# Perceiver block on one core: score maxima from half of the contraction rows, four heads side by side, three iterations a unit, one ring of five PSUM banks

## The chip, the cores and the metric

The kernel runs on one core of one Trainium2 chip. A core has a matrix engine (TensorE, PE in the profile; its weight loads are shown as PEld), a vector engine (VectorE, DVE), a scalar engine (ScalarE, ACT), a general one (GpSimd, POOL) and a queue engine (SyncE, SP) that issues the transfers (DMAs). Each engine takes its instructions in order and waits on semaphores for the others. SBUF is the working memory, with 128 partitions (rows); PSUM takes the results of matmuls, in eight banks of 512 fp32 numbers a partition. The metric is the device time of one execution in microseconds (us). The kernel before took 3726.22 us, the median of three runs (3722.47 to 3727.96).

## What is computed

Two perceiver layers run over `x` (32 batches, 64 latents, width 256). Each begins with a cross attention to a context of 32 x 1601 rows, with 16 heads of 16 numbers; the second one has a mask. Self attentions and feed-forward blocks follow. The part that the change touches is the cross attention:

```
def _L0_xattn_ref(q, k, v, wq, bq, wk, bk, wv, bv, wo, bo):
    qh = (q @ wq + bq).reshape(b, -1, H, HD).transpose(0, 2, 1, 3)
    kh = (k @ wk + bk).reshape(b, -1, H, HD).transpose(0, 2, 1, 3)
    vh = (v @ wv + bv).reshape(b, -1, H, HD).transpose(0, 2, 1, 3)
    scores = jax.nn.softmax(jnp.einsum('bhqd,bhkd->bhqk', qh, kh), axis=-1)
    attn = jnp.einsum('bhqk,bhkd->bhqd', scores, vh)
    concat = attn.transpose(0, 2, 1, 3).reshape(b, -1, H * HD)
    return concat @ wo + bo
...
x = x + _L0_xattn_ref(_layernorm(x, axis=-1), ctx_1024, ctx_1024, ...)
x = x + _L0_attn_ref(...)
x = x + _L0_ffn_ref(...)
x = x + _L1_xattn_ref(_layernorm(x, axis=-1), ctx_1024, mask_BxS2_ik0, ...)
x = x + _L1_attn_ref(...)
x = x + _L1_ffn_ref(...)
```

## The kernel before

The method `stream` does both cross attentions in one loop and puts the smaller blocks of layer 0 between its steps. The order of the instructions is written by hand: what the Python code emits first stands first on each engine.

**Units.** A unit `u` is one batch and four of its heads (`b, q4 = divmod(u, 4)`); with two layers of 32 batches there are 256. For each unit the keys of four heads are fetched, the maximum of each row of scores is found, the exponents of (score minus maximum) are made, and the values are summed with them.

**Exact products from bf16 parts.** A key or a query number is split into three bf16 parts (0, 1, 2, from coarse to fine). The contraction over a head's 16 numbers becomes one over 6 x 16 = 96 rows, which hold six products of parts: `PARTS` says which part of the key each sixth row has, `QPARTS` which part of the query. Row 16 and so on belong together by a step of six: `k[s : 96 : 6]`. Rows from 96 hold constants: ones against the maximum's two bf16 parts, and in layer 1 the mask row.

**What a unit runs**, by the functions that the change touches:

- `fetch(u)` (L1145) loads the key tile `kst` from `kd`, the keys' parts in HBM, with six transfers, one for each sixth row (L1154), and one more for the constant rows (L1158). The pool `kst` has three tiles: `fetch(u + 2)` stands at the head of unit `u` and waits until unit `u - 1` has read its tile.
- `maxima(u)` (L1169) makes the scores once with queries on the partitions: 32 queries of a head in each of four column groups of PE, 96 rows (97 in layer 1), 400 keys to a matmul (L1182). Each set of four fills one bank `sp` (a pool of three), which DVE reduces (L1187). Eight sets make a unit. Then `neg`, `mm` (L1190 to L1192) and a transposing matmul `rp` into a bank of the ring `tp` (L1196), and ACT copies the maxima from there into rows 96 and on of the query tile `qst` (L1200).
- `probabilities(u, i)` (L1206) makes the scores again with keys on the partitions, now with the maximum subtracted by the extra rows (98 or 99 rows), two chunks of 128 keys to a bank `tp` (L1217; a ring of two banks, shared with `rp`), and ACT takes the exponent (L1222). Seven calls make a unit.
- `weighted(u, i, e)` (L1225) sums the values into the bank `acc`, 17 columns of PE to a head (L1232).

**What runs between.** `keys_values` makes the keys and values of later batches, one bank at a time: `kp` (12 matmuls, L1048, evacuated by DVE at L1054) and `vp` (12, L1076, evacuated by ACT at L1081), 13 banks for four units. They use two banks in turn, `mm0` and `mm1`, as do the group and end steps (`group_step`, `end_step`: queries, self attention, the feed-forward block, the finish of a batch pair). `parted` (L989) splits the keys with ACT and POOL and stores them to `kd`; `split` (L939) casts a context tile (`chi`, ACT) and makes its rest (`clo`, POOL). `tick` (L962) emits pending pieces of these, at most two pieces of work at each call, and issues the context loads that were asked for one tick before. All loads and stores go through SP's queue.

**The loop.** A unit has four iterations. Each issues part of the next unit's maxima (3, 3, 3 steps, and in the fourth `rp`), the sums of the iteration before, two exponents' scores, a group step, a tick, projections up to a target, and an end step:

```
for i in range(4):
    for _ in range((3, 3, 3, 0)[i]):
        next(nat, None)
    for done in late:
        weighted(*done)
    ...
    late = [(u, j, probabilities(u, j)) for j in range(2 * i, min(2 * i + 2, 7))]
    ...
    keys_values(LEAD + (4 * u + i + 1) / 16.0, 0.15)
    end_step()
```

**The start.** Before the loop, `stream` loads the first context tiles (six of them into a key tile that is not yet needed, `early`), makes the first queries with a layer norm whose reciprocal root runs on POOL (`rsqrt`, L196), and the keys of batch 0. DVE's cast of the value weights (L204) stands behind that layer norm's L533 in DVE's order.

Of the kernel before, what the change touches and what calls it, by code (L numbers as in the profile page):

```python
# [19 lines left out]
F32 = mybir.dt.float32  # L20
F32R = mybir.dt.float32r
BF16 = mybir.dt.bfloat16
# [19 lines left out]
PARTS = (0, 0, 0, 1, 1, 2)  # L42
QPARTS = (0, 1, 2, 0, 1, 0)
# [15 lines left out]
class Kernel:  # L59
# [188 lines left out]
    def stream_setup(self, wp, bg, bank):  # L248
# [39 lines left out]
        self.eye = wp.tile([P, NQ], F32, tag="eye", name="eye")  # L288
# [7 lines left out]
        self.tri = wp.tile([P, NQ], F32, tag="tri", name="tri64")  # L296
# [34 lines left out]
        for c0 in (0, half):  # L331
# [7 lines left out]
            nc.sync.dma_start(self.rows[:, 0, c0 : c0 + n], mf[:, :n])  # L339
# [134 lines left out]

    def stream(self):
        nc, tc, ins = self.nc, self.tc, self.ins
        with ExitStack() as ctx:
# [6 lines left out]
            kq = pool("kq", 2)  # L484
            kp_ = pool("kst", 3)
            vp_ = pool("v")
            pt = pool("pt", 2)
# [5 lines left out]
            ps_n = pool("psn", 3, space=PSUM)  # L493
            ps_t = pool("pst", 2, space=PSUM)
            ps_m = pool("psm", 1, space=PSUM)
# [3 lines left out]

            self.rows = dram.tile([NB, 3, NKP], BF16, tag="rows", name="rows")  # L500
# [7 lines left out]
            def nrows(b):  # L508

                return (96, 98) if layer(b) == 0 else (97, 99)  # L510


            banks = [0, 0]

            def bank(name):
                banks[0] += 1
                banks[1] ^= 1
                return ps_m.tile([P, 512], F32, tag=f"mm{banks[1]}", name=name)
# [44 lines left out]
            def queries(n, g):  # L563
# [27 lines left out]
                q = kq.tile([P, 16, 2 * P], BF16, tag="qst", name=f"{name}_qst{g}")  # L591
                for s, part in enumerate(QPARTS):
                    nc.sync.dma_start(
                        q[s : 96 : 6], qd[part].rearrange("(h d) n -> d h n", d=16)
                    )
                if n == 1:
                    nc.sync.dma_start(
                        q[96:97],
                        self.rows[0:1, 1, : 2 * P].unsqueeze(1).to_broadcast([1, 16, 2 * P]),
                    )  # L600
# [388 lines left out]
            def parted(i, x, quick):  # L989
# [6 lines left out]
                nc.scalar.copy(ks[:, 0, :, :m], upper(x))  # L996
                eng.tensor_tensor(x, x, upper(x), ALU.subtract)  # L997
# [6 lines left out]
                if not quick:  # L1004

                    yield "wait"
# [134 lines left out]
            mms = [wp.tile([P, 2, 3], BF16, tag=f"mm{r}", name=f"mm_{r}") for r in range(4)]  # L1141
            for mm in mms:
                nc.gpsimd.memset(mm[:, :, 0:1], 1.0)

            def fetch(u):  # L1145

                b, q4 = divmod(u, 4)
# [1195 lines left out]
```

## Time and profile before

| | |
|---|---|
| median of three runs | 3726.22 us |
| the profiled execution | 3724.4 us |
| its span, first to last instruction | 3722.7 us |
| mean granted TensorE clock | 0.959 |
| maxima: `sp` matmuls, L1182 | 8192, 511.9 us busy |
| scores for the exponents: `tp`, L1217 | 13312, 580.3 us |
| sums: `acc`, L1232 | 26624, 580.4 us |
| exponents on ACT, L1222 | 1792, 933.7 us |
| reductions on DVE, L1187 | 2048, 1049.7 us |
| key loads | 1536 of 201.0 KB |

Busy times of PE overlap: its matmuls are pipelined, and those in different column groups run side by side, so the sum of the rows is more than PE's share. For the cost of a group of matmuls the start of one is compared with the start of the next. "Idle before" with a releaser says how long an engine had nothing to do before a group, and what ended that.

By stage:

```
us            PE busy  DVE    ACT    POOL   clock  DMA share
0-60          37.63    31.88  23.50  16.53  0.96   0.62
60-460        380.88   246.42 254.37 191.14 0.97   0.82
1260-1660     391.03   248.93 258.32 194.51 1.00   0.76
2460-2860     385.42   242.29 265.94 214.64 0.99   0.85
2860-3160     283.46   179.42 190.62 146.73 0.97   0.82
3160-3722     418.56   465.24 255.51 162.99 0.81   0.05
```

### The profile page before, as it was taken

To read this page: it belongs to the slowest core of one execution; us is meant where nothing else is said; L and a number is where in the kernel's file an instruction comes from. 1 tells how busy PE (TensorE), PEld (TensorE's weight loads), DVE (VectorE), ACT (ScalarE), POOL (GpSimd) and SP (SyncE) were. 2 spreads that over 40 slices of the span, in tenths; PEclk is the share of its full clock that TensorE was granted. 3 is DMA by queue.
4 is the path that set the end of the run, shared out by engine and by line. 5 is a ranking of instruction groups with operands and counts; after the bars stand their busy time and mean duration, and the time that the engine had idled before them with its cause. 6 is when DMAs were issued, how large, how long until landed. Compare 5 with 4: busy or idle time off the path is not lost. (4 is left out here: it accounts for less than half of the span.)

```text
span 3722.7 us, 154775 instructions
## 1 busy us (share of the span) xinstructions
PE 3471.3 (93%) x66591; PEld 2817.5 (76%) x66591; DVE 2437.7 (65%) x6161; ACT 2290.3 (62%) x4400; POOL 1747.7 (47%) x2113
## 2 busy tenths in 40 slices
PE   7999999999999999999999999999999999675698
PEld 6788888888888888878887888788888787342467
DVE  5666666655665666666766666665656565689879
ACT  4666666666666666666666666566666665244662
POOL 3444445545554445544555555555555553003246
PEclk9999999999999999999999999999999999786699
DMA  7887777777877787867877787778888887200000
GB/s 187 229 222 204 195 192 206 207 189 189 206 191 194 188 207 194 217 176 186 206 191 194 181 200 195 195 190 215 219 211 213 213 220 188 73 1 1 1 5 20
DMA packets 669950, 643.36 MB, mean 173 GB/s; under 512 B 114448, under 2 KB 567376, under 8 KB 669136
## 3 DMA queue, kind: packets, MB, share of 16 engines
q1 hardware_dynamic: 669264, 633.45, 66.6%
q8 instruction: 523, 8.57, 1.0%
q14 instruction: 163, 1.34, 0.1%
HBM read 462.30 MB, written 170.98 MB: 170 GB/s over the span
## 5 line engine op out<-in xcount | busy, mean ns | idle before, releaser
L1187 DVE TENSOR_REDUCE mx<-sp 128x1 f32<-128x400 f32 (+1 forms) x2048 | 1049.7, 566 | 415.9 <-PE sp L1182 412.6
L1222 ACT ACTIVATE e<-tp 128x512 f32<-128x512 f32 (+1 forms) x1792 | 933.7, 566 | 594.7 <-PE tp L1217 585.1
L997 POOL TENSOR_TENSOR kr<-kr 128x512 f32<-128x512 f32 (+1 forms) x406 | 411.8, 1014 | 932.3 <-ACT ks L996 853.3
L1054 DVE TENSOR_SCALAR kr<-kp,bk 128x256 f32<-128x256 f32 (+1 forms) x832 | 356.6, 470 | 546.3 <-PE kp L1048 430.0
L944 POOL TENSOR_TENSOR clo<-raw,chi 128x512 fp32r<-128x512 f32 (+1 forms) x408 | 509.6, 1249 | 415.7 <-ACT chi L943 407.7
L1232 PEld LDWEIGHTS acc<-e,v 128*17 128x17 f32 x26624 | 459.0, 98 | 196.7 <-ACT e L1222 78.3
L1232 PE MATMUL acc<-e,v 128*17 128x64 f32 x26624 | 580.4, 221 | 29.0 <-ACT e L1222 19.5
L1217 PE MATMUL tp<-xa_qst,kst 98*128 98x64 bf16 (+2 forms) x13312 | 580.3, 195 | 0.0
L1182 PE MATMUL sp<-kst,xa_qst 96*32 96x400 bf16 (+3 forms) x8192 | 511.9, 343 | 51.8 <-DMA kst<-kd 19.2
L1217 PEld LDWEIGHTS <-kst 98*128 98x128 bf16 (+2 forms) x13312 | 460.1, 100 | 111.8 <-issue 3.6
L1076 PE MATMUL vp<-w_hi,chi 128*128 128x256 f32 (+1 forms) x1664 | 509.0, 306 | 11.9 <-DVE w_hi L204 9.5
L1076 PE MATMUL vp<-w_lo,chi 128*128 128x256 f32 (+1 forms) x1664 | 471.8, 284 | 0.4 <-DVE w_lo L205 0.3
L1076 PE MATMUL vp<-w_hi,clo 128*128 128x256 f32 (+1 forms) x1664 | 471.0, 283 | 0.0
L998 POOL TENSOR_TENSOR ks<-kr 128x512 bf16<-128x512 f32 (+1 forms) x406 | 412.2, 1015 | 31.8
L1048 PE MATMUL kp<-chi,w_hi 128*128 128x256 f32 (+1 forms) x1664 | 373.1, 306 | 7.1 <-DVE w_hi L204 5.6
L1081 ACT COPY v<-vp 128x512 f32<-128x512 f32 (+1 forms) x416 | 244.4, 587 | 165.7 <-PE vp L1076 155.0
L1076 PEld LDWEIGHTS vp<-w_hi,chi 128*128 128x128 f32 (+1 forms) x1664 | 311.9, 187 | 32.7 <-issue 10.3
L1048 PE MATMUL kp<-chi,w_lo 128*128 128x256 f32 (+1 forms) x1664 | 336.5, 284 | 0.1
L1048 PE MATMUL kp<-clo,w_hi 128*128 128x256 f32 (+1 forms) x1664 | 334.2, 283 | 1.3 <-POOL clo L944 1.3
L996 ACT COPY ks<-kr 128x512 bf16<-128x512 bf16 (+1 forms) x416 | 252.3, 607 | 121.8 <-DVE kr L1054 109.7
L1076 PEld LDWEIGHTS vp<-w_lo,chi 128*128 128x128 f32 (+1 forms) x1664 | 312.3, 188 | 1.5 <-DVE w_lo L205 0.9
L1182 PEld LDWEIGHTS <-xa_qst 96*32 96x32 bf16 (+1 forms) x8192 | 155.5, 95 | 206.6 <-issue 97.4
(721 smaller groups left out, 5245.8 us busy)
## 6 DMA issues: line engine op xcount, KB each, us to landing
kst<-kd SPq DMA_DIRECT2D x1536, 201.0 KB
kd<-ks SPq DMA_DIRECT2D x384, 384.0 KB
raw<-in_ctx_dram SPq DMA_DIRECT2D x379, 256.0 KB
xa_qst<-xa_qd SPq DMA_DIRECT2D x96, 128.0 KB
kd<-ks SPq DMA_DIRECT2D x64, 108.0 KB
xa_qd<-xa_qs SPq DMA_DIRECT2D x16, 384.0 KB
kst<-rows SPq DMA_DIRECT2D x128, 37.7 KB
raw<-in_ctx_dram SPq DMA_DIRECT2D x62, 72.0 KB
```

Source lines behind the costliest of these rows:

```text
L944: (nc.vector if i < 2 else nc.gpsimd).tensor_tensor(lo[:, :, :n], raw[:, :, :n], hi[:, :, :n].bitcast(F32), ALU.subtract)
L996: nc.scalar.copy(ks[:, 0, :, :m], upper(x))
L997: eng.tensor_tensor(x, x, upper(x), ALU.subtract)
L998: eng.tensor_tensor(ks[:, 2, :, :m], x, upper(x), ALU.subtract)
L1048: nc.tensor.matmul(kp[:, oc, :m], wk[w][:, cc, oc * P : (oc + 1) * P], x[:, cc, :m], start=(j == 0), stop=(j == 5),)
L1054: nc.vector.tensor_scalar(r[:, oc, :m], kp[:, oc, :m], self.bk[n][:, oc : oc + 1], None, ALU.add,)
L1076: nc.tensor.matmul(vp[:w_, i1, :], x[:, cc, o], wv[w][:, cc, :], start=(j == 0), stop=(j == 5),)
L1182: nc.tensor.matmul(sp[32 * w : 32 * w + 32, :n], q[:NR, h0 + 2 * p + w // 2, t0 : t0 + 32], k[:NR, 2 * p + w // 2, k0 : k0 + n], start=Tru ...
L1187: nc.vector.tensor_reduce(mx[:, p, g : g + 1], sp[:, :n], AX.X, ALU.max)
L1217: nc.tensor.matmul(sp[:m, c, h, :], k[:NA, h, k0 : k0 + m], q[:NA, h0 + h, tok], start=True, stop=True,)
L1222: nc.scalar.activation(e[:m, :two], sp[:m, :two], AF.Exp)
L1232: nc.tensor.matmul(acc[32 * h : 32 * h + 17, slot, :], vs[b, c][:m, 4 * q4 + h, :], e[:m, c - 2 * i, h, :], start=(c == 0), stop=(c == NCH ...
```

## The change

- The maxima use 64 rows of each head's contraction instead of 96 or 97: three products of parts (0 with 0, 0 with 1, 1 with 0 in an order that differs by half) and the constant rows. Even heads use rows 0 to 63, odd heads rows 64 to 127, so that two heads' products stand in the upper half of PE and two in the lower, in two banks. A quad of matmuls has 64 queries of each of four heads and 400 keys; four quads make a unit. The maxima used for the exponents are then those of the coarser scores.
- The rows of the key and query tiles are laid out anew (`ROWS`, `PARTS`, `QPARTS`): in each half 0 to 31 by twos, 1 to 31 by twos, 35 to 50. Where the even and odd heads need different parts, a load is cut in two. All 128 rows enter the scores for the exponents. Unused rows must be zero and constant rows one, so three key tiles and two query tiles are made once and cleared at the start (two key tiles and the query tiles by POOL; the third key tile's rows by four loads in its first fetch). The mask row is loaded in layer 1 alone.
- The loop has three iterations a unit: two quads in each of the first two, `rp` in the third. Exponents 0 and 1, 3 and 4, 5 and 6 are issued as before; 2 is issued after the first iteration's projections. Group and end steps come before the tick and the projections; the third iteration has a second group step, and in odd units an end step.
- The PSUM pools of three (`sp`) and two (`mm0`, `mm1`) banks become one ring of five; the pool of exponents has three tiles instead of two.
- `parted` takes the first part by a rounding copy instead of the upper half of the bits, and stores one step earlier.

```
-PARTS = (0, 0, 0, 1, 1, 2)
-QPARTS = (0, 1, 2, 0, 1, 0)
+ROWS = [slice(r + a, r + b, c) for r in (0, 64) for a, b, c in ((0, 32, 2), (1, 32, 2), (35, 51, 1))]
+MAXR, MASKR = slice(96, 98), slice(34, 99, 64)
+PARTS = ((0, 0), (0, 2), (1, 1), (0, 0), (2, 0), (1, 1))
+QPARTS = ((0, 2), (1, 0), (0, 1), (2, 0), (0, 1), (1, 0))
...
-            pt = pool("pt", 2)
+            pt = pool("pt", 3)
-            ps_n = pool("psn", 3, space=PSUM)
-            ps_m = pool("psm", 1, space=PSUM)
+            ps_m = pool("psm", 5, space=PSUM)
...
             def bank(name):
                 banks[0] += 1
-                banks[1] ^= 1
-                return ps_m.tile([P, 512], F32, tag=f"mm{banks[1]}", name=name)
+                return ps_m.tile([P, 512], F32, tag="mm", name=name)
...
+                q = qring[g % 2]
+                for x, (r, two) in enumerate(zip(ROWS, QPARTS)):
+                    for a, part in enumerate(two):
+                        nc.sync.dma_start(
+                            parity(q[r])[a],
+                            qd[part].rearrange("(j a d) n -> a d j n", a=2, d=16)[a],
+                        )
+                    if x % 2:
+                        yield
+                nc.sync.dma_start(q[MAXR], q[51:53])
...
-                nc.scalar.copy(ks[:, 0, :, :m], upper(x))
-                eng.tensor_tensor(x, x, upper(x), ALU.subtract)
+                nc.scalar.copy(ks[:, 0, :, :m], x)
+                eng.tensor_tensor(x, x, ks[:, 0, :, :m], ALU.subtract)
...
-                if not quick:
-                    yield "wait"
                 yield "store"
...
+                k = kring[u % 3]
+                if u == 2:
+                    for r in (slice(32, 35), slice(51, 64), slice(96, 99), slice(115, P)):
+                        nc.sync.dma_start(k[r], kring[0][r])
+                for r, two in zip(ROWS, PARTS):
+                    rows = [
+                        kds[b][part, 64 * q4 : 64 * q4 + 64, :NKE] for part in two
+                    ]
+                    if two[0] == two[1]:
+                        nc.sync.dma_start(k[r], rows[0].rearrange("(h d) n -> d h n", d=16))
+                        continue
+                    for a, x in enumerate(rows):
+                        nc.sync.dma_start(
+                            parity(k[r])[a],
+                            x.rearrange("(j a d) n -> a d j n", a=2, d=16)[a],
+                        )
+                if layer(b) == 1:
+                    nc.sync.dma_start(
+                        k[MASKR],
+                        self.rows[b % NB, :NKE].unsqueeze(0).unsqueeze(0)
+                        .to_broadcast([2, 4, NKE]),
+                    )
...
+                for g, (k0, n) in enumerate(NATGROUPS):
+                    sp = [bank(f"sp{u}_{a}_{g}") for a in range(2)]
+                    for a in range(2):
+                        r = slice(64 * a, 64 * a + 64)
+                        for j in range(2):
                             nc.tensor.matmul(
+                                sp[a][64 * j : 64 * j + 64, :n], q[r, h0 + 2 * j + a, tok],
+                                k[r, 2 * j + a, k0 : k0 + n], start=True, stop=True,
                             )
+                    for a in range(2):
+                        nc.vector.tensor_reduce(
+                            mx[:, a, g : g + 1], sp[a][:, :n], AX.X, ALU.max
+                        )
+                    if g < 3:
                         yield
...
+            for k in kring[:2]:
+                nc.gpsimd.memset(k, 0.0)
+                nc.gpsimd.memset(k[MAXR], 1.0)
+            for q in qring:
+                nc.gpsimd.memset(q, 0.0)
+                for a in range(2):
+                    nc.gpsimd.memset(
+                        q[32 + 64 * a : 35 + 64 * a].rearrange("p (j a) n -> p j a n", a=2)[:, :, a],
+                        1.0,
+                    )
...
-                for i in range(4):
-                    for _ in range((3, 3, 3, 0)[i]):
+                for i, js in enumerate(((0, 1, 2), (3, 4), (5, 6))):
+                    for _ in range((2, 2, 0)[i]):
                         next(nat, None)
...
-                    if i == 3:
+                    if i == 2:
                         next(nat, None)
-                    late = [
-                        (u, j, probabilities(u, j)) for j in range(2 * i, min(2 * i + 2, 7))
-                    ]
+                    late = [(u, j, probabilities(u, j)) for j in js[:2]]
                     banks[0] = 0
                     group_step()
+                    end_step()
                     tick()
-                    keys_values(LEAD + (4 * u + i + 1) / 16.0, 0.15)
-                    end_step()
+                    keys_values(LEAD + (3 * u + i + 1) / 12.0, 0.15)
+                    late += [(u, j, probabilities(u, j)) for j in js[2:]]
+                    if i == 2:
+                        group_step()
+                        if u % 2:
+                            end_step()
```

## The prediction

> **What bounds the kernel now.** I read the page's busy shares first, then the busy time by windows, then what TensorE (PE) waits for, then one unit on the timeline. A unit is one batch and four heads; the main loop runs 256 of them.
>
> ```profile
> PE 3471.3 (93%) x66591; PEld 2817.5 (76%) x66591; DVE 2437.7 (65%) x6161; ACT 2290.3 (62%) x4400; POOL 1747.7 (47%) x2113
> 860.00:1260.00 400.00, 394.61 (x8045) 326.53 (x8043) 251.47 (x592) 260.17 (x522) 198.57 (x225) 0.99 0.76 196
> ```
>
> In the window (its columns: PE, PEld, DVE, ACT, POOL, granted clock, DMA share, GB/s) PE is busy 394.6 of 400 us, DVE 63%, ACT 65%, the DMA engines 76%. The loop runs from the first maxima at 57.85 us to about 3,172 us: 3,114 us / 255 = 12.2 us a unit. PE sets it. The remaining 550 us are not edited.
>
> ```profile
> L1182 PE MATMUL sp<-kst,xa_qst 96*32 96x400 bf16 (+3 forms) x8192 | 511.9, 343 | 51.8 <-DMA kst<-kd 19.2
> 1002.19 0.28 PE L1196 MATMUL rp<-identb,mm 128*2 128x128 bf16 x2
> 1002.40 0.32 PE L1217 MATMUL tp<-xa_qst,kst 98*65 98x64 bf16 x4
> ...
> 1004.16 0.70 PE L1182 MATMUL sp<-kst,xa_qst 96*32 96x401 bf16 x12
> 1004.69 0.28 PE L1232 MATMUL acc<-e,v 65*17 65x64 f32 x8
> 1004.91 0.64 PE L1217 MATMUL tp<-xa_qst,kst 98*128 98x64 bf16 x16
> ```
>
> The timeline's first columns are start and length. Matmuls overlap, so I cost them by start to next start. Twelve `sp` take 4.16 to 4.69, 0.53 us: 0.177 us for each set of four side by side. From `tp` to `sp` costs about 0.09 us more than staying in `tp` (start to start 123 ns against 29), from `acc` to `tp` as much.
>
> **The quads (gain).** Before, 8 sets of four a unit; after, 4 quads of 64x64 tiles, two row halves by two column halves. Do four such tiles overlap? L1629 is the same arrangement (both row halves, both column halves, two banks):
>
> ```profile
> L1629 PE MATMUL sa_dm<-sa_qk 64*64 64x64 bf16 x512 | 9.3, 228 | 8.5 <-DVE sa_mxd L1638 6.8 <-ACT sa_fi@s L1597 1.7
> ```
>
> Its starts in the trace come in fours within some 15 ns, a new four every 53 ns, so they do overlap, and 53 ns of weight loading hides under a 400-column stream. I take 0.177 us a quad: 4 x 0.177 = 0.71 us a unit, x255 = -181 us. Bounds: nothing (halves in turn) to -181. Mode switches: eight a unit before (in and out, four iterations); after, three in each of two iterations (into `sp`, `sp` to `acc`, out) and two in the third, eight again: nothing. `tp` on 128 rows instead of 98 costs nothing: 98 and 99 rows both go at 29 ns.
>
> **Wait A (cost).** The third iteration now issues `rp`, `tp` 5, `tp` 6. All three draw on the two-bank ring, so `tp` 6 needs the bank that `rp` filled, and ACT must copy it out first (L1200, 366 ns). Before, `rp` was followed by `tp` 6 alone. From the second `rp` matmul's start to the end of that copy the trace has 622 ns; ACT to a waiting PE takes 52. PE arrives at 149 (`rp` to `tp`) + 8 x 29 = 381. Stall 674 - 381 = 0.29 us a unit: +75 us (0 to 90). Queued behind it on PE are the projections and the next unit's maxima.
>
> **Wait B (cost).** `tp` 2 moves behind the projection and its exponent is used one `sp` run later. If a value projection came just before (97 of 256 units by the changed instruction order), ACT evacuates `vp` first: 904 ns after the last `vp` start, + 597 (mean exponent) + 52 = 1.55 us. PE arrives after 120 + 326 (`tp` 2 and switch) + 177 + 256 (quads, switch) + 416 (32 `acc`) = 1.30. Stall 0.26 x 97 = +25 us. After a key projection the two arrive together; I add 0.08 x 144 = 12. Sum +37 (0 to 100, if ACT has a copy queued in every unit).
>
> **Waits that go (gain).**
>
> ```profile
> PE acc L1232 <- ACT e L1222: 15.5, 28, 1.6
> ...
> PEld acc L1232 <- ACT e L1222: 70.5, 186, 1.8
> ```
>
> `acc` waits on exponents mostly where an iteration has no projection (72 of some 770). With 13 banks over 12 iterations instead of 16 nearly each has one. By start-to-start excess these stalls are 38 us; I take -25 (0 to -38). The three-bank `sp` ring costs some 22 us beside DMA waits; the five-bank ring frees -10 (0 to -22). VectorE's eight 566 ns reductions stay, 4.5 us a unit, in two bursts of four (2.3 us) inside iterations of some 3.9 us; `neg` and `mm` follow and are needed 0.3 to 0.8 us later, behind the key projection's 0.9 us evacuation if there is one. I cost that at nothing; with the cover gone it is 0.3 us a unit.
>
> **Start (cost).** GpSimd (POOL) now clears two key and two query tiles before its first useful instruction.
>
> ```profile
> L302 POOL MEMSET v<- 128x1024 f32 x1 | 1.0, 957 | 0.0
> L282 POOL MEMSET blk<- 128x128 f32 x1 | 0.2, 203 | 0.0
> ...
> 12.89 0.24 POOL L196 TENSOR_SCALAR xa_rs_v<-xa_mv 128x2 f32<-128x2 f32 x1 [10.22 <-DVE xa_mv L527]
> ...
> 16.20 0.58 PE L1076 MATMUL vp<-w_hi,chi 128*128 128x256 f32 x1 [7.51 <-DVE w_hi L204]
> ```
>
> (957 - 203) / 896 = 0.84 ns an element and about 0.1 us each. 4 x 6,432 + 2 x 4,096 + 4 x 2,048 = 42,112 elements: 35.4 + 1.0 = 36.4 us, from 2.66 to 39. The first layer norm's L196 waited only until 12.89; behind it stand, in order, DVE's L533, the cast that the first `vp` waits for, and PE. +26 us. No row has bf16 on POOL; at a quarter of the price it is hidden, so 0 to +29. Twice as many query loads at 0.63 us on SP before the first key load: 0 to +4, I take 2. Start: +28.
>
> The Trainium skill ("VectorE: DVE Perf Modes", "Zero memsets can be issued as uint32 (trn2)") says that a memset takes a cycle an element whatever the type, and that zeros can go as 4-byte words; it speaks of the Vector engine. If that were done here, the zero tiles would halve and the start cost some 18 us.
>
> **Loads (cost, and the largest doubt).**
>
> ```profile
> 1002.75 4.01 SPq L1154 DMA_DIRECT2D kst<-kd  x6
> 1006.81 0.44 SPq L1158 DMA_DIRECT2D kst<-rows  x1
> 1007.36 0.93 SPq L1009 DMA_DIRECT2D kd<-ks  x1
> ```
>
> A unit's key tile goes from 6 loads and one for rows to 8, and a mask load in layer 1: 4.5 us of SP becomes 5.4 to 6.0, and stores and context loads behind it come later. The packets end 7.1 us after the first issue (8.0 with the rows); the maxima that read them start a median 3.8 us after that. So the loads themselves stay hidden. Context loads lose cover too: three ticks a unit instead of four put the cast of a load 0.79 units after its issue point, not 0.98 (positions in the two instruction orders): 9.6 us becomes the cover instead of 12, with the issue some 1 us later. Query loads, 12 and one instead of 6 every 16 units, pass SP in groups of four, 2.5 us each, within the 3.8. I take +20 us for the units where ACT or PE then waits (0 to +100).
>
> The rounding copy L996 now reads 512 fp32 elements, as L943 does (0.62 us against 0.61), and POOL's subtraction reads that copy: nothing, as both have idle time. Group and end steps move ahead of the projections on PE: the same work in another order, nothing.
>
> **Sum.** -181 + 75 + 37 - 25 - 10 + 28 + 20 = -56. The profiled execution took 3,724.4 us (3,722.7 span and 1.7 around it), 1.8 below the median. 3,726 - 56 = 3,670 us.
>
> **Rivals.** (1) Key loads become the bound: slower. Before, each load wrote 16 partitions six apart over 96; now 16 two apart within 32, or 16 adjacent ones. For it: the 3,216-byte packets take 127 ns at best but 201 in the mean, 245 at the upper quartile and 515 in the worst hundredth, so something shared slows them. Against: in the first load all 16 engines run at 127 ns together. With 245 for the four spread groups and 515 for the two adjacent ones the mean is 335 ns: 384 x 0.134 / 16 = 3.2 us more engine time a unit. Now it is 0.78 x 12.2 = 9.5; 12.7 exceeds any PE time: 255 x 0.5 + 28 = 3,880 us. It decides from some 300 ns a packet; at 310 a unit takes 9.5 + 24 x 0.109 = 12.1 us, little gain is left, and with the start the time is about 3,740.
>
> The skill's "SBUF — State Buffer", section "Door 1: The DMA port swizzle (why `[64,N]` ≈ `[32,N]`)", speaks for this rival: bandwidth goes by how many of 16 ports the partitions reach, four adjacent ones sharing one, with about 436 GB/s over all. An estimate from it: 0.95 us for a spread group (8 ports), 1.9 us for an adjacent one (four rows on a port), 7.6 us a unit against 4.8 now; engine time 12.3 us, and the whole 3,780. The burst at 127 ns contradicts it for pairs; nothing here shows four on a port.
>
> (2) ACT's order takes the place of the gain: the raw loads' shorter cover blocks casts at the head of ACT's queue, exponents stand behind, PE waits 0.4 us a unit more: +82 beyond the 20, 3,750 us, slower. For it: ACT is in order and waits A and B hang on it; against: `vp`'s copy starts 37 ns after its matmuls at the 75th percentile, so ACT seldom lags.
>
> (3) Waits A and B hidden: 3,726 - 181 - 35 + 28 = 3,540; with A alone gone 3,670 - 75 = 3,595. Against: A is the same bank in every unit.
>
> (4) The quads do not overlap: 3,670 + 181 = 3,850. Against it L1629.
>
> **How the numbers follow.** Likeliest: the sum, 0.50, own range 3,610 to 3,715; rival 1 0.17, rival 2 0.17, rival 3 0.11, rival 4 0.05. No change means within 0.2%, 7.5 us, about what a measurement can tell. Faster: 0.46 of the likeliest, 0.11 of rival 3, 0.01 of rival 2: 0.58. Same: 0.03 + 0.02 + 0.03 = 0.08. Slower 0.34. The range 3,570 to 3,790 takes in rival 2, part of 1 and part of 3.
>
> **What would show it.** `sp` rows at 4,096 matmuls with some 250 us busy; `tp` waiting for ACT `xa_qst` or `qst` in each unit, 0.3 us; `acc` waiting for `e` after `vp`; POOL memsets to about 39 us and the first `vp` near 42; 3,216-byte packets still near 200 ns. Wrong: packets past 300 ns and a DMA share of 0.95, or POOL free by 13 us, or units under 11.6 us.

## The result, and the profile after

The changed kernel takes 3846.38 us, the median of four runs (3840.5 to 3850.63), beside 3727.09 us for the kernel before in the same session: a ratio of 1.0316, 95% interval 1.0291 to 1.0341. It is 3.2% slower. The prediction was 3,670 us, faster; the time lies above its range (3,570 to 3,790), and the sign is the other one.

First the page: busy times and the row of the DMA queue, then the groups that answer to those shown before.

```profile
PE 3370.9 (88%) x62481; PEld 2741.0 (71%) x62495; DVE 2420.7 (63%) x6161; ACT 2288.6 (59%) x4400; POOL 1830.1 (48%) x2119
...
q1 hardware_dynamic: 676848, 628.95, 75.8%
...
L1229 PE MATMUL tp<-qst,kst 128*128 128x64 bf16 (+1 forms) x13312 | 624.8, 196 | 61.0 <-ACT qst L1213 22.6
...
L1191 PE MATMUL sp<-kst,qst 64*64 64x400 bf16 (+1 forms) x4096 | 328.6, 354 | 168.7 <-DMA kst<-kd 78.7
...
L949 ACT CAST chi<-raw 128x512 fp32r<-128x512 f32 (+1 forms) x410 | 249.5, 608 | 156.7 <-DMA raw<-in_ctx_dram 156.5
```

PE is busy for 100 us less than before, in a run that is 126 us longer. The maxima are what was promised, 4,096 matmuls and 329 us instead of 8,192 and 512. But 169 us of idle time stand ahead of them (52 before), mostly until key loads land, 61 us ahead of the scores (none before), and ACT's cast of the context tiles now waits 157 us for transfers (37 before). The DMA queue's packets take 75.8% of 16 engines' span, though it moves slightly less (628.95 MB, before 633.45 at 66.6%): each packet has become slower. The rows of the kernel before that answer to these:

```profile
q1 hardware_dynamic: 669264, 633.45, 66.6%
...
L1217 PE MATMUL tp<-xa_qst,kst 98*128 98x64 bf16 (+2 forms) x13312 | 580.3, 195 | 0.0
...
L943 ACT CAST chi<-raw 128x512 fp32r<-128x512 f32 (+1 forms) x410 | 249.5, 609 | 36.9 <-DMA raw<-in_ctx_dram 36.8
```

The same in the loop: the window that the prediction showed, for the kernel after (columns PE, PEld, DVE, ACT, POOL, granted clock, DMA share, GB/s), and then the busiest waits of PE in the window 400 to 2,800 us (us in total, times, longest).

```profile
860.00:1260.00 400.00, 371.25 (x7399) 308.59 (x7402) 244.51 (x576) 255.71 (x511) 205.21 (x221) 0.98 0.88 188
```

```profile
PE sp L1191 <- DMA kst<-kd: 33.9, 13, 5.2
PE sp L1191 <- DMA kst<-rows: 23.1, 7, 8.2
PE tp L1229 <- ACT qst L1213: 15.5, 37, 0.9
PE sp L1191 <- DMA raw<-in_ctx_dram: 13.7, 5, 5.2
```

PE was busy for 394.6 of these 400 us before, now for 371.3, at nearly the same clock (0.99 and 0.98); the DMA share went from 0.76 to 0.88. The waits for loads are few and long, up to 8 us: it is not every unit that is late, but some.

**Where the time went.** By the trace the loop ran from 57.86 to 3,189.9 us before, 12.235 us a unit, and runs from 85.64 to 3,314.8 after, 12.614 a unit: +27.8 us at the start, +97 over the 256 units, +1.4 behind them. I split the 97 further. The excess of a PE instruction is how much later it starts after the one before it than the median of all such pairs in that loop (the same two lines of the kernel; within one line, the same place in the row of matmuls, for `sp` in the set of four).

```
us over the loop                       before   after   difference
excess ahead of sp (maxima)               67      218     +151
excess ahead of tp (exponents' scores)    16      120     +104
excess ahead of acc (sums)                72       53      -19
excess ahead of kp, vp, rp                40       84      +44
all excess                               210      493     +283
the loop without its excess             2922     2736     -186
```

So the four quads gave their 180 us, and nine tenths of what took them away are two rows: PE waits at the maxima for loads, and at the scores for ACT. The loop without its excess is a steady measure: 2,922 us again in run b3 below, which has the same matmuls as the kernel before, and 2,747 and 2,740 in e1 and e3, which have those of the changed kernel.

By what stands ahead of the late starts (idle time of PE over 150 ns, and what ended it), the 283 are: transfers, at the maxima, +127 (35 before, 162 after); ACT and shorter waits at the scores, +86; DVE, +28; idle time that ends with nothing the profile shows, which it calls "issue", +27 (3 and 30). Another +28 (38 and 66) is matmuls without idle time that are slow where the granted clock is 0.5, which it is for 97 us of the loop before and 214 after. The rest is -13.

### The profile page after: what moved, and what is told of

Same layout as the page of the kernel before. It is cut to its first block, busy times and chain, and to the rows that moved or that the text cites. A ratio compares the mean times of both kernels' runs of the same rounds, so it can differ in the third digit from the quotient of the medians.

```text
span 3848.9 us, 146881 instructions
## 1 busy us (share of the span) xinstructions
PE 3370.9 (88%) x62481; PEld 2741.0 (71%) x62495; DVE 2420.7 (63%) x6161; ACT 2288.6 (59%) x4400; POOL 1830.1 (48%) x2119
## 3 DMA queue, kind: packets, MB, share of 16 engines
q1 hardware_dynamic: 676848, 628.95, 75.8%
## 5 line engine op out<-in xcount | busy, mean ns | idle before, releaser
L1196 DVE TENSOR_REDUCE mx<-sp 128x1 f32<-128x400 f32 (+1 forms) x2048 | 1031.6, 564 | 431.9 <-PE sp L1191 431.6
L1003 POOL TENSOR_TENSOR kr<-kr,ks 128x512 f32<-128x512 f32 (+1 forms) x406 | 459.9, 1133 | 705.4 <-ACT ks L1002 636.4
L1229 PE MATMUL tp<-qst,kst 128*128 128x64 bf16 (+1 forms) x13312 | 624.8, 196 | 61.0 <-ACT qst L1213 22.6
L1229 PEld LDWEIGHTS <-kst 128*128 128x128 bf16 (+1 forms) x13312 | 484.9, 100 | 182.1 <-issue 89.9
L1244 PE MATMUL acc<-e,v 128*17 128x64 f32 x26624 | 546.4, 223 | 18.8 <-issue 10.3
L1244 PEld LDWEIGHTS acc<-e,v 128*17 128x17 f32 x26624 | 399.0, 98 | 224.6 <-issue 166.0
L1191 PE MATMUL sp<-kst,qst 64*64 64x400 bf16 (+1 forms) x4096 | 328.6, 354 | 168.7 <-DMA kst<-kd 78.7
L949 ACT CAST chi<-raw 128x512 fp32r<-128x512 f32 (+1 forms) x410 | 249.5, 608 | 156.7 <-DMA raw<-in_ctx_dram 156.5
L1079 PEld LDWEIGHTS vp<-w_hi,clo 128*128 128x128 f32 (+1 forms) x1664 | 314.4, 189 | 0.0
```

The source lines that it names most:

```text
L949: nc.scalar.copy(hi[:, :, :n], raw[:, :, :n])
L1003: eng.tensor_tensor(x, x, ks[:, 0, :, :m], ALU.subtract)
L1079: nc.tensor.matmul(vp[:w_, i1, :], x[:, cc, o], wv[w][:, cc, :], start=(j == 0), stop=(j == 5),)
L1191: nc.tensor.matmul(sp[a][64 * j : 64 * j + 64, :n], q[r, h0 + 2 * j + a, tok], k[r, 2 * j + a, k0 : k0 + n], start=True, stop=True,)
L1196: nc.vector.tensor_reduce(mx[:, a, g : g + 1], sp[a][:, :n], AX.X, ALU.max)
L1229: nc.tensor.matmul(sp[:m, c, h, :], k[:, h, k0 : k0 + m], q[:, h0 + h, tok], start=True, stop=True,)
```

## The experiments

All times are medians, and each ratio is to the kernel before in the same session (3,723 to 3,729 us there); the changed kernel's 3,846 us is the mark for what is built on it. The names (e1 and so on) are those of the runs. Packet figures are those of the 3,216-byte packets that carry the key rows. A key fetch is called late if its first transfer is issued over 1 us after its slot came free (units 30 to 219). e1, e2 and b3 leave key loads out, so that some rows keep old keys, and e5 and e5b put another part of the key into two row groups: these five are measurements, not versions of the kernel.

### Are the adjacent rows the cause? Two loads left out (e1, e2)

```
for x, (r, two) in enumerate(zip(ROWS, PARTS)):
+   if u > 2 and x in (2, 5):      # e1; (0, 3) in e2
+       continue
```

> The changed kernel, but from the fourth unit on the two key loads into 16 adjacent rows (35 to 50 and 99 to 114) are left out, so those rows keep old keys: 128 of a unit's 384 packets fewer. Port theory (adjacent rows make slow packets, and the DMA engines become the bound): the slow ones go, the remaining 3,216-byte packets take about 200 ns in the mean as in the kernel before, the DMA share of the loop falls from some 0.93 to 0.65, and the time falls to about 3,690 us (3,650 to 3,730). Rival (three iterations a unit press ACT's copies and the shorter cover of the context loads sets the time; DMA is only a passenger): 3,846 +- 25 us, though DMA has less to do.

Measured: 3,645.37 us, ratio 0.978 (0.9765 to 0.9798); packets 177 ns in the mean, DMA share of the window 400 to 2,800 us 0.60.

> The changed kernel, but from the fourth unit on the two key loads into rows two apart that hold the first part in both halves (rows 0, 2, .. 30 and 64, 66, .. 94) are left out: as many packets and bytes fewer as in the run without the adjacent ones. Port theory: the slow packets stay, the mean of the remaining ones rises to some 285 ns or more, the DMA share falls only to about 0.80, and the time is 3,700 to 3,790, 10 to 60 us above the run without the adjacent ones. If adjacency does not matter and only the count of packets does, the two runs have the same packet mean and agree within 10 us. Rival (ACT and the three iterations): 3,846 +- 25.

Measured: 3,694.54 us, ratio 0.990 (0.9887 to 0.9917); packets 246 ns, share 0.74. The rival with ACT is out: with less to load, 201 and 152 us go. As many bytes and issues are left out in both, so the 49 us between them are the adjacency. The larger part, 152, is not.

The group of e1 that answers to the cast above, and its maxima:

```profile
L949 ACT CAST chi<-raw 128x512 fp32r<-128x512 f32 (+1 forms) x410 | 249.5, 608 | 57.8 <-DMA raw<-in_ctx_dram 57.8
...
L1193 PE MATMUL sp<-kst,qst 64*64 64x400 bf16 (+1 forms) x4096 | 310.3, 347 | 38.9 <-DMA kst<-kd 21.8
```

The 169 us of idle time ahead of the maxima are 39 here, the 157 us ahead of the cast 58.

A control: two loads left out of the kernel before (b3).

```
for s, part in enumerate(PARTS):
+   if u > 2 and s in (0, 3):
+       continue
```

> A control. The kernel before, but from the fourth unit on two of the six key loads are left out (first and fourth of every six rows keep old keys; the three key tiles are named instead of taken from a pool). In the changed kernel leaving out two loads gave 201 or 152 us; part of that could be a gain that fewer loads bring to any version. If the loads of the kernel before are hidden, as the prediction held: 3,715 to 3,728 us, and the 201 us are the change's own. If it too waits for loads (its waits of sp for transfers are 17 us in a window of 2,400): 3,690 to 3,710, and so much less is the change's.

Measured: 3,668.27 us, ratio 0.985 (0.9829 to 0.9866). Both theories missed it: the kernel before gains 55 us too. Loads were not hidden there. Of the 201 us some 146 are then the change's own, near the +151 of the table. With loads out of the way in both, the loop takes 11.815 us a unit against 12.006. That is 23 us between the two runs (3,645 and 3,668), the start included: without the loads the change does gain, but not the 76 us to which the prediction's other terms add up.

### The price of adjacency by itself

The kernel before with other rows and nothing else changed, the query tile's rows likewise (b1):

```
-   k[s : 96 : 6]
+   k[16 * s : 16 * s + 16]
```

> The kernel before with nothing changed but the rows of the key and query tiles: each of the six key loads writes 16 adjacent rows instead of 16 rows six apart. Port theory (four adjacent rows share one way into the memory): 3,216-byte packets go from 201 ns to some 450 to 500 ns, the engines need 384 x 0.475 / 16 = 11.4 us a unit for them instead of 4.8, some 16 us with the rest, and the time is 4,500 to 4,800 us. If the changed kernel's packets are slow because eight loads are on the way at once: 201 ns and 3,727 us.

Measured: 4,585.45 us, ratio 1.2304 (1.2243 to 1.2364). Packets 363 ns in the mean (201 before), upper quartile 454, worst tenth from 488. The window 400 to 2,800 us, in the kernel before and then in b1:

```profile
400.00:2800.00 2400.00, 2351.45 (x48242) 1957.73 (x48241) 1520.23 (x3620) 1565.61 (x3127) 1229.52 (x1433) 0.99 0.78 198
```

```profile
400.00:2800.00 2400.00, 2056.44 (x38443) 1691.20 (x38444) 1213.48 (x2903) 1255.70 (x2499) 965.06 (x1108) 0.91 0.92 157
```

The engines are taken for 0.92 of the time and move 157 GB/s, against 0.78 and 198 for the kernel before: the rows alone cost 859 us. The Trainium skill ("SBUF — State Buffer", "Door 1: The DMA port swizzle (why `[64,N]` ≈ `[32,N]`)") says that four adjacent rows share a port; the prediction's estimate from it, 1.9 us for such a load, is 475 ns for each of its 64 packets on 16 engines. The slowest quarter (454 and more) comes near that; the mean, 363, is a quarter below it.

Most of the 859 us is not late keys. PE's longest waits in the same window (us in total, times, longest):

```profile
PE acc L1232 <- issue: 115.1, 51, 5.1
PE tp L1217 <- issue: 68.9, 30, 6.3
PE kp L1048 <- issue: 31.4, 15, 4.9
PE sp L1182 <- DMA kst<-kd: 20.3, 5, 7.9
```

PE's gaps of the kind "issue" are 288 us of these 2,400, beside 3 in the kernel before. The profile also shows a queue for instructions, q8, which brings one packet of 16 KB for each 256 of PE's matmuls and weight loads (302 packets for 77,315 in this window). 133 of the 135 gaps end 1.2 to 2.0 us after the latest packet of that queue has ended; 10% of all moments lie so. PE thus seems to run out of instructions that come late among the slow packets; no run tests this by itself. Of the 831 us by which the excess grows over the loop, 497 are such gaps, 246 matmuls at a granted clock of 0.5, and 84 waits for transfers at the maxima.

### The rows two apart

The changed kernel with all its products, its two adjacent groups moved (e3):

```
-ROWS = [slice(r + a, r + b, c) for r in (0, 64) for a, b, c in ((0, 32, 2), (1, 32, 2), (35, 51, 1))]
+ROWS = [slice(a, b, 2) for a, b in ((0, 32), (1, 32), (32, 64), (64, 96), (65, 96), (98, 128), (99, 100))]
...
```

> The changed kernel with all its products, but the two adjacent groups moved to rows two apart (32, 34, .. 62 and 98, 100, .. 126 with one row, 99, by itself; mask rows 35 and 101): one load of one row more a unit. Port theory: packets back near 200 ns in the mean, DMA share about 0.80, time 3,690 us (3,650 to 3,740). If only the count of loads or the three iterations matter: 3,846 us or some us more.

Measured: 3,807.10 us, ratio 1.021 (1.0193 to 1.0224). The packets did what was expected, 191 ns and a share of 0.71, below the kernel before; the time did not, only 39 us of it went. Over the loop the excess for transfers at the maxima is 53 us less than in the changed kernel and that of the kind "issue" 25 less (30 to 5), but PE's waits for ACT at the scores are 28 more. The slow packets were one limit, and another stands close behind it.

### SP's queue

Fewer issues with the same packets (e5):

> The changed kernel with the four half loads of a unit put together to two whole ones (first part for even and odd heads alike, so two of the six row groups hold another part than the changed kernel's): six key loads a unit on SP's queue instead of eight, the same bytes, packets, rows and row spacing. Theory Q (SP's queue: the run of key issues has grown from 4.1 to 5.6 us and everything behind it, stores, context loads, the next fetch, comes later): a unit loses about 0.4 to 0.6 us, 3,700 to 3,750 us. Theory D (the DMA engines' time on the slow packets): packets and share stay, 3,846 +- 20 us.

```
-PARTS = ((0, 0), (0, 2), (1, 1), (0, 0), (2, 0), (1, 1))
+PARTS = ((0, 0), (0, 0), (1, 1), (0, 0), (0, 0), (1, 1))
```

Measured: 3,902.70 us, ratio 1.047 (1.0454 to 1.0493), 56 us slower than with eight loads. Theory Q fails here: the run of issues shrinks from a median 5.6 to 4.0 us, yet the last packet still lands 9.6 us after the first issue (9.7 with eight), since the packets are no faster (269 ns after 255, share 0.90). Theory D did not foresee a loss either. The loss is not at the maxima, where the excess is 22 us less, but in PE's gaps of the kind "issue", as in b1: 54 of them with 56 us in the window 400 to 2,800 us, against 19 with 16 us in the changed kernel, all but one ending 1.2 to 2.0 us after the latest packet of the instruction queue. Over the loop they are 61 us more. The largest group, in the changed kernel and then in e5:

```profile
PE acc L1244 <- issue: 10.1, 12, 1.7
```

```profile
PE acc L1244 <- issue: 29.3, 24, 2.6
```

Why six whole loads bring more of them than eight stays open.

For the second limit I looked at which instructions stand on SP while a key fetch is late. The timeline of SP in the changed kernel at one such unit (start, length):

```profile
796.11 3.40 SPq L599 DMA_DIRECT2D qst<-xa_qd  x4
799.62 0.53 SPq L442 DMA_DIRECT2D wid<-L_attn_w_qkv_r  x1
...
800.67 2.16 SPq L599 DMA_DIRECT2D qst<-xa_qd  x4
802.92 1.44 SPq L937 DMA_DIRECT2D raw<-in_ctx_dram  x1
804.48 1.00 SPq L1012 DMA_DIRECT2D kd<-ks  x2
805.52 2.38 SPq L599 DMA_DIRECT2D qst<-xa_qd  x4
807.95 0.65 SPq L606 DMA_DIRECT2D qst<-qst  x1
808.71 0.59 SPq L1160 DMA_DIRECT2D kst<-kd  x1
```

The slot was free at 798.05; the fetch begins at 808.71, behind twelve query loads and one more, two stores, a context load and two transfers of weights (one of them under the dots). The maxima that need it start at 815.28, and that unit takes 18.6 us. Of 190 fetches 56 are late in the changed kernel, 296 us in sum, 79 us of that query loads; before it was 20, 89 and 24.

The query loads to another queue, in e3 (f1):

> The kernel with the rows two apart (e3_rows_apart, 3,807 us, DMA share 0.71), with the query loads (12 and one every 16 units) issued from GpSimd's queue instead of SP's. In that kernel 64 of 190 key fetches start over 1 us after their slot is free, and 95 of the 335 us of that lateness is query loads at the head of SP's queue. Theory Q2 (with the slow packets gone, SP's queue is the next limit): lateness falls by about a third and the time to 3,765 to 3,790 us. If SP's queue is covered: 3,807 +- 15. If GpSimd is hurt by the issuing: above 3,820.

```
-   nc.sync.dma_start(parity(q[r])[a], ...)
+   nc.gpsimd.dma_start(parity(q[r])[a], ...)
```

Measured: 3,731.73 us, ratio 1.001 (0.9993 to 1.0029): 75 us less than with the rows alone, more than expected. The lateness falls from 335 to 136 us. GpSimd's group of these issues (busy, mean ns of one, idle before):

```profile
L600 POOL DMA_DIRECT2D qst<-xa_qd x168 | 92.0, 555 | 10.5 <-DMA qst<-xa_qd 4.8 <-DMA xa_qd<-xa_qs 3.4 <-issue 2.3
```

92 us of GpSimd in 2,400, and hardly a wait in front of it.

The same edit with the adjacent rows still there (a1):

> The changed kernel with only the query loads moved to GpSimd's queue; the adjacent rows stay. It tells whether the slow packets matter once SP's queue is shorter. Two limits that take turns: the packets keep the DMA share near 0.9 and the time falls less than the 75 us that the same edit gave with the rows apart: 3,790 to 3,830. If SP's queue is the only limit: 3,771 (the same 75 us less) or below, and the rows would be worth nothing by themselves.

Measured: 3,804.52 us, ratio 1.021 (1.0183 to 1.0229). Four kernels now form a square:

```
                        adjacent rows   rows two apart
query loads on SP            3846            3807
query loads on GpSimd        3805            3732
```

Each edit alone gives about 40 us, both 115. It is not that the waits at the maxima go only when both are repaired: the excess for transfers there is 162 us, 109 with the rows, 92 with the queue and 66 with both, less than the two gains added. The difference is in other rows of PE: its waits for ACT at the scores are 34, 62, 36 and 36 us, and the excess at a granted clock of 0.5 is 66, 66, 65 and 45. What links these to the loads I did not test.

And in the kernel before (b2):

> A control. The kernel before with its query loads (6 or 7 every 16 units) issued from GpSimd's queue. Of its 89 us of late key fetches in 190 units 24 us are query loads at the head of SP's queue, against 79 in the changed kernel. If that edit pays only where the change has doubled the query loads: 3,715 to 3,727 us. If it pays as much here: 3,650 to 3,690, and the changed kernel with all four edits has no advantage of its own.

Measured: 3,719.25 us against 3,723.47, ratio 0.999 (0.9977 to 1.0004). In the kernel before the same edit brings nothing that can be told from zero: it repairs what the change did.

Fewer issues once more, with the rows apart (e5b):

> The kernel with the rows two apart, and the four half loads put together to two whole ones (first part for both parities, so two row groups hold another part): seven key issues a unit instead of nine, same bytes and rows. With the slow packets still there the same edit lost 56 us. Theory Q2: with the engines free the shorter issue (6.6 to some 5.2 us a fetch) counts: 3,720 to 3,770 us. If what the two left-out loads bring in the first two runs is bytes and not issues: 3,807 or more.

Measured: 3,757.06 us, ratio 1.008 (1.0051 to 1.0105), within the expectation: with the rows apart, two issues fewer a unit give 50 us, where they had lost 56 beside the slow packets.

The pause before the key stores (e6):

> The changed kernel with the pause between ACT's second key copy and the key stores put back, as the kernel before had it. If the store that stands at the head of SP's queue and waits for that copy (218 us in 2,400 on SP, with key loads behind it) is what makes fetches late: 3,780 to 3,820 us, and late first issues (over 1 us after the slot is free: 56 of 190 units now) become fewer. If the queue's length or the packets matter alone: 3,846 +- 15.

```
    nc.scalar.copy(ks[:, 1, :, :m], upper(x))
+   if not quick:
+       yield "wait"
    yield "store"
```

Measured: 3,864.09 us, ratio 1.037 (1.035 to 1.0384), nothing gained. SP's waiting for that copy is not what makes fetches late.

### The three iterations and the row of maxima

Four iterations again (e4):

> The changed kernel with four iterations a unit again (two exponent tiles in each of three, one in the fourth; the row of maxima in the fourth, 16 shares of projections a unit); rows, quads, five-bank ring and start as in the changed kernel. Port theory: DMA still sets the unit, 3,830 us (3,800 to 3,860), the share still above 0.85 and TensorE's waits for key loads still over 100 us. Rival (three iterations): the wait of the third tile for ACT's copy goes, as does the context loads' shorter cover, and the time falls to 3,700 to 3,760.

```
-for i, js in enumerate(((0, 1, 2), (3, 4), (5, 6))):
+for i, js in enumerate(((0, 1), (2, 3), (4, 5), (6,))):
```

Measured: 3,867.30 us, ratio 1.037 (1.0354 to 1.0385). Three iterations are not the cause; four are 21 us worse.

The row of maxima later (e7):

> The changed kernel with the row of maxima moved behind the projections of the third iteration, so that the seventh exponent tile no longer needs the bank that it used. The prediction's wait A: by the trace 70 us of excess ahead of tp in a window of 2,400, some 90 us over the loop. If the waits add up: 3,755 us (3,740 to 3,775). If the key loads set the pace of a unit and PE's own waits lie inside that: 3,820 to 3,850.

```
     if i == 2:
-        next(nat, None)          # before the exponents' scores
...
     if i == 2:
+        next(nat, None)          # behind the projections
         group_step()
```

Measured: 3,814.16 us, ratio 1.023 (1.0216 to 1.0248). The excess ahead of `tp` falls from 120 to 46 us over the loop, but 32 us come back: between the two theories. Half of the 74 is paid on PE itself: the loop without its excess grows from 2,736 to 2,772 us. Behind the projections `rp` stands between two more changes of matmul: from `kp` or `vp` to `rp` takes 209 ns from start to start and from `rp` to `sp` 148, where from `acc` to `rp` took 56, and from `kp` or `vp` to `sp` 210.

### Put together

Rows, maxima row and start (c1):

> The kernel with the rows two apart, the row of maxima behind the projections of the third iteration, and a cheaper start: constants written as 4-byte words, the first key and query tile cleared after the first layer norm's work has been queued on GpSimd, the second pair after the first fetch. Same results as the changed kernel. If the parts add: 3,807 - 32 to 90 (maxima row) - 15 to 27 (start): 3,690 to 3,760 us. If late keys take up what the row gives: 3,770 to 3,790.

```
-   nc.gpsimd.memset(k, 0.0)
-   nc.gpsimd.memset(k[MAXR], 1.0)
+   nc.gpsimd.memset(flat(k), 0.0)             # flat: the tile as fp32 words
+   nc.gpsimd.memset(flat(k[MAXR]), ONES)      # two bf16 ones in a word
```

Measured: 3,756.33 us, ratio 1.007 (1.0047 to 1.0098). The first maxima start at 67.7 us instead of 86.6, 18.9 of the 51 us; the other 32 are the row's.

With the query and context loads on GpSimd (c2):

> The former kernel, with the query loads and the context loads of the loop issued from GpSimd's queue. Theory Q2: SP's issues a unit fall by some 2.5 (9 key loads, 2 stores stay), fetches start on time, and the time is 3,640 to 3,710 us, the first correct version below the kernel before. If GpSimd's issuing delays its own subtractions and so the keys: at or above the former kernel.

Measured: 3,745.02 us, ratio 1.003 (1.0015 to 1.0051), a miss: only 11 us.

With the query loads alone there (g1):

> The changed kernel with four edits: key and query rows two apart, query loads issued from GpSimd, the row of maxima behind the projections of the third iteration, the cheaper start. If the parts add: 3,732 (rows and queries together) - 18 (start, by the first maxima at 67.7 instead of 86.6 us) - 32 to 75 (row): 3,660 us (3,635 to 3,685), 1 to 2.5% below the kernel before. If something else now sets the unit: 3,700 to 3,715, the start alone.

Measured: 3,689.05 us, ratio 0.990 (0.9878 to 0.9915), 1% below the kernel before, and the fastest version that leaves nothing out. It is the former without the context loads on GpSimd, so these cost 56 us there: PE's waits for `clo`, which GpSimd makes behind them, are 34.1 us in 2,400 with them and 17.8 without, and its waits for exponents ahead of the scores 26.8 and 0.6. It is a little above the expectation because the start gives 8 us here instead of 19: on GpSimd the first query loads (50.5 to 58.2 us) and the second clearing (to 69.9) now stand ahead of a `clo` for which PE waits 17.6 us. Its window and its `tp` row, the latter for 400 to 2,800 us:

```profile
860.00:1260.00 400.00, 388.11 (x7816) 321.17 (x7814) 262.17 (x600) 272.64 (x545) 230.30 (x262) 1.00 0.75 202
```

```profile
L1230 PE MATMUL tp<-qst,kst 128*128 128x64 bf16 (+1 forms) x10256 | 443.5, 195 | 6.0 <-ACT qst L1214 4.3 <-ACT e L1235 0.6 <-PE tp L1230 0.3
```

PE is busy for 388 of 400 us again, the DMA share is back at 0.75, and the wait ahead of `tp` is 6 us (38.2 in the changed kernel's same window).

The same with four iterations (g3):

> As the first kernel of this call (rows apart, queries on GpSimd, cheaper start), but with four iterations a unit as in the kernel before, so that the row of maxima is followed by one exponent tile and needs no move. It tells what three iterations are worth by themselves once the loads are out of the way: by the prediction's terms nearly nothing (waits that go -35, wait B +37): within 15 us of the first kernel. Above it by 20 us or more: three iterations are a gain; below: a cost.

Measured: 3,714.33 us, ratio 0.997 (0.9954 to 0.998), 25 us above the three iterations: they are a gain by themselves, about as large as beside the slow loads (21).

## Why the prediction was wrong

**The step that failed is "Loads (cost, and the largest doubt)".** It took 20 us, with 100 as the upper end; the table shows 151 us more excess ahead of the maxima, and the control leaves 146 us of the 201 that two left-out loads give. Three things in that step were wrong.

*The cover was read wrongly, and in the middle instead of at its edge.* "The maxima that read them start a median 3.8 us after that": 3.8 us is the lower quartile of that time over all units. The median is 5.3, and one unit in twenty has 1.9 or less. "So the loads themselves stay hidden" does not follow from either; b3 shows that even before they were not. After the change the lower quartile is 1.6 us, and one unit in twenty has nothing left (it starts 0.2 us before the last packet, which its first two matmuls, on rows 0 to 63, do not need).

*The query loads were held to be covered.* "In groups of four, 2.5 us each, within the 3.8" looked at one group. They meet key loads, stores and context loads on the same queue, three groups one behind the other, and in the unit shown the fetch came 10.7 us late.

*The packets' price was mistaken for a threshold.* Rival 1 named the mechanism, the adjacent rows, and priced it at 335 ns a packet, deciding from 300. Measured were 255, below the point: 384 x 0.054 / 16 = 1.3 us more engine time a unit, 10.8 in all, less than a unit. By that rule it should have cost nothing, and it cost 39 to 49 us. A share of 0.88 to 0.89 is a mean over units: what counts at the maxima is when the last packet of a late fetch lands, and part of the price, 25 us between the changed kernel and e3, is PE's gaps of the kind "issue", for which the prediction had no term. The chance of 0.17 went to an all-or-nothing version of what happened in part.

**The other terms**, measured against the same table:

- *The quads* (-181): 186 us less of PE's own time. Within a run of eight matmuls the second four start 184 ns after the first four: they overlap, rival 4 is out.
- *Wait A* (+75): +104 us of excess ahead of `tp`, 11 of it of the kind "issue". The mechanism was right, but it was not worth as much: removing it gave 32 us beside the slow packets, 32 with the rows apart (c1 less its start) and 35 in the best version (3,732 - 3,689 = 43, less 8 for the start). The excess ahead of `tp` fell by 74 us each time that I can compare (e7 with the changed kernel, g1 with f1), and `rp`'s new place cost 36 and 39 us of PE's own time.
- *Wait B and the waits that go* (+37 and -25): -19 us ahead of `acc` together, 12 predicted.
- *The ring of `sp`* (-10): not to be told from the loads' waits at the same place.
- *`kp`, `vp`, `rp`* were costed at nothing: +44 us. Of these 19 are waits for DVE, 6 for GpSimd's `clo`, and 14 matmuls at a granted clock of 0.5. Rival 2's own sign, PE waiting for exponents because ACT's casts wait, is small: 6 us of such waits in 2,400 at the scores and sums, 9 before.
- *The start* (+28): 27.8.

The largest miss is the first: 151 us at the maxima where loads and ring were to bring 20 - 10. Wait A and the row of `kp`, `vp`, `rp` add 29 and 44, and the row of `acc` takes off 31.

The timeline for the start, GpSimd and then PE, in the changed kernel:

```profile
2.46 5.46 POOL L1312 MEMSET kst<- 128x6432 bf16 x1
7.98 5.62 POOL L1313 MEMSET kst<- 2x6432 bf16 x1
...
35.51 3.63 POOL L1317 MEMSET qst<- 3x2048 bf16 x2
39.24 0.24 POOL L201 TENSOR_SCALAR xa_rs_v<-xa_mv 128x2 f32<-128x2 f32 x1
...
42.55 0.58 PE L1079 MATMUL vp<-w_hi,chi 128*128 128x256 f32 x1 [31.07 <-DVE w_hi L209]
```

6,432 elements in 5.46 us are 0.85 ns each, and the first `vp` starts at 42.55 instead of 16.20.

Still open: whether late instruction packets are what ends PE's gaps of the kind "issue", as their times suggest, why six whole loads bring more of them than eight (e5), and how the two edits of the square gain more together than one by one.

## What to carry to other kernels

Whether a load is hidden is not read from the median of its cover but from the units with the least, and the test is cheap: leave a load out of the kernel before and see if its time falls. When a layout is changed for the matmuls, look at what it does to the transfers in both of their currencies, the rows that one transfer writes together and the issues that its queue must pass; here repairing one gave 40 us and both together 115. The price of slow transfers need not show as a wait for a load: in b1 most of it showed as idle time of PE without a named cause. And an issue-bound queue is relieved by moving the rare, bunched loads to an engine off the path, not those that feed that engine's own work.

## What the runs showed of the hardware

- Sixteen rows written by one load: six apart 201 ns a packet (the kernel before), two apart but for one row 191 (e3, half loads among them) or 223 (e5b, whole loads), adjacent 363 (b1), all in the mean. In e3 a quarter of the packets take 127 ns, in b1 a quarter less than 312.
- GpSimd clears 2 partitions of 6,432 bf16 numbers in 5.62 us, 128 of them in 5.46, and as 3,216 fp32 words in 2.8 us either way:

```profile
14.97 2.78 POOL L1317 MEMSET kst<- 128x3216 f32 x1
17.81 2.80 POOL L1318 MEMSET kst<- 2x3216 f32 x1
```

The Trainium skill ("VectorE: DVE Perf Modes", "Zero memsets can be issued as uint32 (trn2)") states for zeros on the Vector engine that 4-byte words pay, as a memset takes a cycle an element whatever the type; the two lines, from the start of c1, show it for GpSimd, and for ones as well as zeros.
- A query load's issue takes 555 ns of GpSimd in the mean (f1), 656 ns of SP's queue (the changed kernel).
- PE's idle time without a named cause ("issue"), in the window 400 to 2,800 us, was at most 5 us in the runs whose DMA share there was 0.80 or less, 8 to 18 us in the changed kernel, a1, e4, e6 and e7 (0.89 to 0.90), 56 in e5 (0.90) and 288 in b1 (0.92).
